# Layer 1 of a graph-network stack: the running-sum table built and read in two column ranges, both rows of a node in one gather

## The chip, the core and the metric

The kernel runs on one core of one Trainium2 chip. TensorE (PE) multiplies, VectorE (DVE), ScalarE (ACT) and GpSimd (POOL) do the element-wise work, SyncE (SP) and POOL issue transfers, and sixteen DMA engines move bytes between the chip's memory and on-chip memory. Each engine works through its own instructions in order and waits for the others by semaphores. The metric is the time on the device in microseconds, as the median of several runs.

## The reference, cut to what matters

Four graph layers run over 2708 nodes with 128 features each, all with the same adjacency matrix. Each begins with a layer norm and a relu, and adds to the residual `x`. The change is in layer 1 alone:

```python
XW = X @ W
s_col = XW @ a[0, :128];  s_row = XW @ a[0, 128:]
den = exp(leaky_relu(s_row[:, None] + s_col[None, :], 0.01))   # 2708 x 2708
num = A @ den
att = where(num != 0, den / num, 0)
H = A @ (att @ XW)
```

The product `A @ den` is the heavy part. Since `den[i, j]` is one exponential where `s_row[i] + s_col[j]` is positive and another where it isn't, column `j` of `num` is a sum over the nodes with a row term above a threshold, and another sum over those below. With the nodes sorted by `s_row` both come out of running sums over sorted rows of the adjacency matrix.

## The kernel before

The adjacency matrix comes in transposed (`adjT`), as rows of 2708 f32 values. Nodes go in 22 tiles of 128 (the last has 20), columns in six banks of 512 (the last has 148).

**Sorting.** The kernel counts for every node how many nodes lie ahead of it, writes pairs (node, row term) to their places in a list in memory (`order_d`), and reads the list back as `srtT`. The node numbers become the indices `src_u`.

**The table stage (L1492 to L1517).** Tile t of the running-sum table needs 126 rows of `adjT` in sorted order. `fetch` (L1399) gathers them with an indirect transfer that POOL issues, into one of four buffers `mov`, three tiles ahead. Rows 0 and 1 of a buffer carry the two running sums on from the tile before. For each bank TensorE multiplies the weights `wt` of the tile (128 x 128) with `mov` (L1498); VectorE copies the first two rows of the product from the accumulator into the next tile's buffer (L1502); and ScalarE, or VectorE for two of the six banks, copies the whole product to `knots` (L1503), which SP writes to the table in memory (L1515). One more column (2708) holds a running sum of weights. In the same loop ScalarE counts signs for the places of the nodes (`signs_of`, L1359), computes the weights of later tiles (L1458), and TensorE computes `xw` = XW (L362). The order of TensorE, VectorE and ScalarE here is partly pinned, partly chosen by a scheduler.

**The last pass (L1615 to L1627).** It starts when the whole table is written. For each node tile POOL gathers two table rows for each node, one below its threshold and one above (`lo` and `hi`, L1538), with one indirect transfer each. `interpolation` (L1546) computes a factor from the last column, `divided` (L1576) combines the rows on VectorE (L1584) and inverts the result on ScalarE by a logarithm and an exponential (L1588, L1589). One tile later `weighed` (L1591) multiplies by the numerator on VectorE (L1596), and TensorE accumulates the product with `xw` over all tiles in six banks (L1606).

**After it.** The accumulators are copied to `yT`, turned and scaled to `attended` (L1640), and `aggregate` (L370, products at L382) multiplies with `adjT` once more, whose rows SP loads in `chunk`s of one tile. The buffers of these chunks are those of `lo` and `mov`.

## Time and profile before

| What | Value |
|---|---|
| median of 3 runs | 1142.2 us (1142.18 to 1153.88) |
| the profiled execution's own time | 1143.4 us |
| its span, first to last instruction | 1141.7 us |
| mean granted TensorE clock | 0.947 |
| busy share of the span: PE, DVE, ACT, POOL | 88%, 53%, 36%, 21% |
| first product of the table stage (L1498) | 477.9 us |
| last table rows landed, first row gather issued | 640.3 us |
| first product of the last pass (L1606) | 661.7 us |
| last product of the last pass ends | 814.1 us |
| first product of the aggregation after it (L382) | 819.4 us |

The profile is one execution. Times of single instructions come from it, and the changed stretch is the 342 us between 477.9 and 819.4. In a table of groups each row is a line of the kernel, an engine and an operation, with count, busy time, mean duration in ns and the idle time before it with its cause. In a table of windows each row gives the busy time of the engines in one stretch, then the clock that TensorE was granted (1.00 is full speed), the mean share in which DMA engines had packets, and the bytes moved. Idle time of an engine that isn't the bound costs nothing.

### The profile page before, as it was taken

To read this page: it belongs to the slowest core of one execution; us is meant where nothing else is said; L and a number is where in the kernel's file an instruction comes from. 1 tells how busy PE (TensorE), PEld (TensorE's weight loads), DVE (VectorE), ACT (ScalarE), POOL (GpSimd) and SP (SyncE) were. 2 spreads that over 40 slices of the span, in tenths; PEclk is the share of its full clock that TensorE was granted. 3 is DMA by queue.
4 is the path that set the end of the run, shared out by engine and by line. 5 is a ranking of instruction groups with operands and counts; after the bars stand their busy time and mean duration, and the time that the engine had idled before them with its cause. 6 is when DMAs were issued, how large, how long until landed. Compare 5 with 4: busy or idle time off the path is not lost. (4 is left out here: it accounts for less than half of the span.)

```text
span 1141.7 us, 10167 instructions
## 1 busy us (share of the span) xinstructions
PE 1008.4 (88%) x3501; PEld 491.5 (43%) x3501; DVE 608.9 (53%) x1248; ACT 414.4 (36%) x660; POOL 237.5 (21%) x208
## 2 busy tenths in 40 slices
PE   7989999999989979777787177787999999999998
PEld 5444444443444455334343033333444455545444
DVE  4374369999823489366576389998500131122003
ACT  5010145555200267568574358877200130012000
POOL 2000000000477715411110447771000000000000
PEclk9989999999999979999899668888999999999999
DMA  9978120004598239799999799998599447725821
GB/s 288 348 269 265 38 80 1 1 29 166 217 388 355 53 112 408 232 367 409 367 375 374 261 424 424 422 413 342 227 383 321 177 148 254 280 98 180 307 98 49
DMA packets 52293, 284.00 MB, mean 249 GB/s; under 512 B 7535, under 2 KB 18918, under 8 KB 29794
## 3 DMA queue, kind: packets, MB, share of 16 engines
q1 hardware_dynamic: 37986, 188.96, 44.7%
q0 software_dynamic: 14016, 94.39, 21.6%
q8 instruction: 28, 0.46, 0.2%
q14 instruction: 23, 0.19, 0.0%
q10 hardware_dynamic: 240, 0.00, 0.0%
HBM read 250.98 MB, written 32.87 MB: 249 GB/s over the span
## 5 line engine op out<-in xcount | busy, mean ns | idle before, releaser
L1606 PE MATMUL acc<-hi,xw 128*128 128x512 f32 (+3 forms) x264 | 126.1, 641 | 55.2 <-DVE hi L1596 55.2
L382 PE MATMUL acc<-chunk,h 128*128 128x512 f32 (+1 forms) x384 | 148.0, 542 | 0.0
L1498 PE MATMUL acc<-mov,wt 128*128 128x512 f32 (+1 forms) x264 | 113.4, 582 | 32.9 <-DMA mov<-in_adj_dram,src_u 31.9
L900 POOL DMA_INDIRECT gath<-ydr,near_u x84 | 80.4, 957 | 191.5 <-issue 179.3
L779 PE MATMUL acc<-zT 128*128 128x512 f32 (+2 forms) x264 | 112.3, 559 | 0.0
L1606 PEld LDWEIGHTS acc<-hi,xw 128*128 128x128 f32 (+1 forms) x264 | 56.2, 222 | 125.1 <-issue 67.4
L1502 DVE COPY mov<-acc 2x512 f32<-2x512 f32 x126 | 74.2, 611 | 58.3 <-PE acc L1498 57.8
L382 PEld LDWEIGHTS acc<-chunk,h 128*128 128x128 f32 x384 | 68.8, 190 | 74.1 <-issue 74.1
L1498 PEld LDWEIGHTS acc<-mov,wt 128*128 128x128 f32 x264 | 51.1, 201 | 95.1 <-issue 71.6
L382 PE MATMUL acc<-chunk,y 128*128 128x512 f32 x204 | 79.9, 552 | 5.9 <-DMA chunk<-in_adj_dram 5.2
L794 ACT COPY strip<-acc 128x512 f32<-128x512 f32 (+1 forms) x132 | 60.4, 558 | 59.2 <-issue 35.8
L382 PE MATMUL acc<-chunk,attended 128*128 128x512 f32 x192 | 73.1, 542 | 2.8 <-DMA chunk<-in_adj_dram 2.8
L1503 ACT COPY knots<-acc 128x512 f32<-128x512 f32 x88 | 50.2, 588 | 56.3 <-DVE mov L1502 52.3
L1588 ACT ACTIVATE hi<-hi,lam 128x2708 f32<-128x2708 f32 (+3 forms) x24 | 56.5, 2363 | 35.0 <-issue 25.6
L796 DVE MAX8 top_v<-strip 128x8 f32<-128x2708 f32 (+1 forms) x22 | 64.6, 2963 | 7.3 <-ACT strip L794 7.3
L1538 POOL DMA_INDIRECT lo<-table,lo_u x22 | 55.2, 2511 | 61.8 <-issue 36.0
L1584 DVE SCALAR_TENSOR_TENSOR hi<-lo,lam,hi 128x2708 f32<-128x2708 f32 (+3 forms) x24 | 67.0, 2800 | 1.0
L779 PEld LDWEIGHTS acc<-zT 128*128 128x128 f32 (+1 forms) x264 | 45.1, 185 | 51.3 <-issue 43.8
L1596 DVE SCALAR_TENSOR_TENSOR hi<-row_all,inv_s,hi 128x2708 f32<-128x2708 f32 (+3 forms) x24 | 67.0, 2797 | 0.4 <-ACT hi L1589 0.4
L382 PEld LDWEIGHTS acc<-chunk,y 128*128 128x128 f32 x204 | 37.4, 193 | 48.4 <-issue 45.4
L1589 ACT ACTIVATE hi<-hi,hb 128x2708 f32<-128x2708 f32 (+3 forms) x24 | 56.5, 2362 | 0.7
L1362 ACT ACTIVATE sg<-row_all,c_nat 128x2708 bf16<-128x2708 f32 (+1 forms) x22 | 56.2, 2555 | 0.1
(323 smaller groups left out, 1280.6 us busy)
## 6 DMA issues: line engine op xcount, KB each, us to landing
chunk<-in_adj_dram SPq DMA_DIRECT2D x74, 1354.0 KB
table<-knots SPq DMA_DIRECT2D x20, 1354.5 KB
res<-in_adj_dram SPq DMA_DIRECT2D x9, 1354.0 KB
held<-in_adj_dram SPq DMA_DIRECT2D x11, 512.0 KB
held<-in_adj_dram SPq DMA_DIRECT2D x16, 256.0 KB
upper<-in_adj_dram SPq DMA_DIRECT2D x4, 842.0 KB
held<-in_adj_dram SPq DMA_DIRECT2D x3, 1024.0 KB
chunkY<-in_adj_dram SPq DMA_DIRECT2D x2, 1354.0 KB
```

What stands on the lines that cost most here:

```text
L382: nc.tensor.matmul(out[b][:, :n], y[r, i, :], chunk(i)[r, k0 : k0 + n], start=(i == 0), stop=(i == T - 2),)
L779: mm = nc.tensor.matmul(zz[b][:w, :n], zT[:, cols(t)], zT[:, k0 : k0 + n], start=True, stop=False)
L794: copied = nc.scalar.copy(s[:w, k0 : k0 + n], zz[b][:w, :n])
L796: nc.vector.max(top_v[:w, t, :], s[:w, :])
L900: nc.gpsimd.indirect_dma_start(out=g[: idx.shape[0], :], out_offset=None, in_=ydr[:, :], in_offset=bass.IndirectOffsetOnAxis(ap=idx, axis=0),)
L1498: nc.tensor.matmul(p[:, :n], wt[:, t, :], moving[t][:, k0 : k0 + n], start=True, stop=True)
L1502: nc.vector.tensor_copy(moving[t + 1][:2, k0 : k0 + n], p[:2, :n])
L1584: nc.vector.scalar_tensor_tensor(num, lo[:w, c], kap, num, op0=ALU.mult, op1=ALU.add)
L1588: nc.scalar.activation(num, num, AF.Ln, scale=sc)
L1589: nc.scalar.activation(num, num, AF.Exp, scale=-1.0, bias=hb40[:w, t : t + 1])
L1596: nc.vector.scalar_tensor_tensor(att[:w, c], row_all[:w, c], inv_s[:w, t : t + 1], att[:w, c], op0=ALU.max, op1=ALU.mult,)
L1606: nc.tensor.matmul(py[b][:, :n], xw[:w, t, :], att[:w, k0 : k0 + n], start=(t == T - 1), stop=(t == T - 2),)
```

## The change

The table is cut at column 1535 into two tables. The first covers columns 0 to 1534 and the column of weight sums (1536 wide), the second the other 1173 columns (1176 wide). Three stretches take the place of the table stage and the last pass.

1. The table stage runs over the first range alone: 22 tiles, three banks each. ScalarE copies bank 0 and VectorE banks 1 and 2. The two carried rows are copied from `knots`, no longer from the accumulator. Signs are counted here, five tiles ahead.
2. A loop over 22 tiles builds the second range's table (ScalarE copies two banks, VectorE the last of 152 columns). From its tile 3 on it issues gathers from the first table, and from its tile 6 on it does one item of the last pass: division ahead of the tile's knots, inversion and the weighing of the item before behind them. An item is a node tile in one range.
3. The other items, six of the first range and all 22 of the second, follow in a loop of their own, with gathers three items ahead.

A node's two table rows now always lie one after the other (each table tile has three carried or repeated rows, so a tile covers 125 nodes and no longer 126), and one indirect transfer brings both, as a row of twice the width. The index of a node's place is computed by rounding, no longer by comparison with all tile starts. All of these instructions are pinned in program order. The first range's half of `yT` and two groups of `attended` are computed inside the third stretch, and the first four chunks of the next aggregation go to new buffers that are free once the second table is made. The scaling and exponential of `row_all` stand between stretches 1 and 2. In front, a row of zeros is set after the indices are known, and the list is read back in two transfers.

```diff
-PER = P - 2
+PER = P - 3
...
-    big = ctx.enter_context(tc.tile_pool(name="big", bufs=4))
+    big_open = ExitStack()
+    big = big_open.enter_context(tc.tile_pool(name="big", bufs=4))
...
+    CUT = 3 * 512 - 1
+    PARTS = ((0, CUT, CUT + 1), (CUT, N, 4 * (-(-(N - CUT) // 4))))
+    WIDE = max(w for _, _, w in PARTS)
+    tables = [
+        dram.tile([P * (T - 1) + LAST, w], F32, name=f"table{h}") for h, (_, _, w) in enumerate(PARTS)
+    ]
...
-    first = row_place()
-    pin(nc.vector.memset(first[0:1, :N], 0.0))
-    nc.vector.memset(first[:, N : N + 1], 0.0)
-    nc.vector.memset(first[0:1, N : N + 1], 1.0)
...
-    for t in range(4):
+    for t in range(5):
...
-    nc.gpsimd.dma_start(srtT[:, 2:, :], order_d[: T * PER, :].rearrange("(t f) c -> t f c", f=PER))
+    for a_, e_, c in ((1, 1 + T * PER, slice(3, P)), (0, T * PER, slice(2, 3))):
+        nc.gpsimd.dma_start(
+            srtT[:, c, :],
+            order_d[a_:e_, :].rearrange("(t f) c -> t f c", f=PER)[:, : c.stop - c.start, :],
+        )
...
+    l1.close()
+    rows_open.close()
+    big_open.close()
+    made = ExitStack()
+    moved = made.enter_context(tc.tile_pool(name="moved", bufs=4))
+    knots = made.enter_context(tc.tile_pool(name="knots", bufs=3))
+    moving = {}
+    tots = keep.tile([P, QUARTER], F32, name="tots", tag="own")
...
+    def fetch(h, t):
+        c0, c1, w = PARTS[h]
+        n = c1 - c0
+        m = moving[h, t] = moved.tile([P, WIDE], F32, name="mov", tag="mov")
+        if t == 0:
+            dve.memset(m[0:1, :n], 0.0)
+        dve.memset(m[:, n:w], 0.0)
+        if t == 0 and h == 0:
+            dve.memset(m[0:1, n:w], 1.0)
+        pin(
...
+    def total_row(h):
+        c0, c1, _ = PARTS[h]
+        for g in range(4):
+            a_, e_ = max(c0, QUARTER * g), min(c1, QUARTER * (g + 1))
...
+    def make_knots(h, t, bank, on_act):
+        m = moving.pop((h, t))
+        o = knots.tile([P, WIDE], F32, name="knots", tag="knots")
+        p = [acc(bank + x_) for x_, _, _ in pieces(h)]
+        for x_, a_, e_ in pieces(h):
+            pe.matmul(p[x_][:, : e_ - a_], wt[:, t, :], m[:, a_:e_], start=True, stop=True)
+        for x_, a_, e_ in pieces(h):
+            if x_ in on_act:
+                act.copy(o[:, a_:e_], p[x_][:, : e_ - a_])
+        for x_, a_, e_ in pieces(h):
+            if x_ not in on_act:
+                dve.tensor_copy(o[:, a_:e_], p[x_][:, : e_ - a_])
+            if t < T - 1:
+                dve.tensor_copy(moving[h, t + 1][:2, a_:e_], o[:2, a_:e_])
+        n = P if t < T - 1 else LAST
+        w = PARTS[h][2]
+        pin(nc.sync.dma_start(tables[h][t * P : t * P + n, :], o[:n, :w]))
+
+    def ahead_fetch(h, t):
+        if t < T:
+            fetch(h, t)
+        elif h == 0:
+            fetch(1, t - T)
+            if t == T:
+                total_row(1)
+
     for t in range(T):
-        if t + 3 < T:
-            fetch(t + 3)
-        o = rowtile("knots")
-        for b, (k0, n) in enumerate(EKBS):
-            p = acc(b)
-            nc.tensor.matmul(
-                p[:, :n], wt[:, t, :], moving[t][:, k0 : k0 + n], start=True, stop=True
-            )
-            if t < T - 1:
-                nc.vector.tensor_copy(moving[t + 1][:2, k0 : k0 + n], p[:2, :n])
-            (nc.vector.tensor_copy if b in (2, 5) else nc.scalar.copy)(o[:, k0 : k0 + n], p[:, :n])
-        if t + 4 < T:
-            signs_of(t + 4)
-        if t == T - 4:
+        ahead_fetch(0, t + 3)
+        make_knots(0, t, 3 * (t % 2), (0,))
+        if t + 5 < T:
+            signs_of(t + 5)
+        if t == T - 5:
             row_places()
         if t % 4 == 0 and t // 4 + 1 < NG:
             weights(t // 4 + 1)
         if t % 3 == 2 and t // 3 < NG:
-            node_product(hT, wg, t // 3, keep_xw, behind=True)
-        s0 = 0 if t else 2
-        if t < T - 1:
-            for c in (slice(0, HALF), slice(HALF, N + 1)) if t == 0 else (slice(0, N + 1),):
-                nc.sync.dma_start(table[t * P + s0 : (t + 1) * P, c], o[s0:, c])
-    for c in (slice(0, HALF), slice(HALF, N + 1)):
-        nc.sync.dma_start(table[(T - 1) * P : (T - 1) * P + LAST, c], o[:LAST, c])
-
-
-    pin(nc.vector.tensor_scalar(row_all, row_all, rmax, 0.99, op0=ALU.subtract, op1=ALU.mult))
-    pin(nc.scalar.activation(row_all, row_all, AF.Exp, bias=forty))
+            weighted(t // 3)
...
+    dve.tensor_scalar(row_all, row_all, rmax, 0.99, op0=ALU.subtract, op1=ALU.mult)
+    act.activation(row_all, row_all, AF.Exp, bias=forty)
...
+    pairs = between.enter_context(tc.tile_pool(name="pairs", bufs=4, side="right"))
+    atts = between.enter_context(tc.tile_pool(name="atts", bufs=4, side="right"))
...
+    def gather(h, t):
+        w, n = width(t), PARTS[h][2]
+        r = pairs.tile([P, 2 * WIDE], F32, name="pair", tag="pair")
+        rows[h, t] = r[:, :n], r[:, n : 2 * n]
+        pin(
+            nc.gpsimd.indirect_dma_start(
+                out=r[:w, : 2 * n],
+                out_offset=None,
+                in_=tables[h][:, :],
+                in_offset=bass.IndirectOffsetOnAxis(ap=pair_u[:w, t : t + 1], axis=0),
+            )
...
+    ORDER = [0, T - 1, *range(1, T - 1)]
+    SETS = {0: (0,), T - 1: (T - 1,), **{t: (t, t + 1) for t in range(1, T - 1, 2)}}
+    WORK = [(h, t) for h in range(2) for t in ORDER]
+    gathers, work = list(WORK), list(WORK)
...
+    def divided(h, t):
+        w = width(t)
+        if h == 0 and t in SETS:
+            interpolation(SETS[t])
+        lo, hi = rows.pop((h, t))
+        at = attention[h, t] = atts.tile([P, WIDE], F32, name="att", tag="att")
+        for c in cuts(h, t):
+            dve.scalar_tensor_tensor(
+                at[:w, c], lo[:w, c], kap[:w, t : t + 1], hi[:w, c], op0=ALU.mult, op1=ALU.add
+            )
...
+    def weighed(h, t):
+        w = width(t)
+        at = attention.pop((h, t))
+        c0, c1, _ = PARTS[h]
+        for c in cuts(h, t):
+            dve.scalar_tensor_tensor(
+                at[:w, c],
+                row_all[:w, c0 + c.start : c0 + c.stop],
+                inv_s[:w, t : t + 1],
+                at[:w, c],
+                op0=ALU.max,
+                op1=ALU.mult,
+            )
+        if h not in py:
+            py[h] = [acc(3 * h + x_) for x_ in range(3)]
...
+    waiting = []
+    for t in range(T):
+        if t + 3 < T:
+            fetch(1, t + 3)
+        if t >= 3:
+            gather(*gathers.pop(0))
+        now = work.pop(0) if t >= 6 else None
+        if now:
+            divided(*now)
+        make_knots(1, t, 3, (0, 1))
+        if now:
+            inverted(*now)
+        if waiting:
+            weighed(*waiting.pop())
+        if now:
+            waiting.append(now)
+    made.close()
...
-    sets = [(T - 1,)] + [(t,) for t in range(3)] + [(t, t + 1) for t in range(3, T - 1, 2)]
-    assert sets[-1][-1] == T - 2
-    before = []
-    for ts in sets:
-        for t in ts:
-            fetch_rows(t)
-        interpolation(ts)
-        for t in ts:
-            divided(t)
-            if before:
-                weighed(before.pop())
-            before.append(t)
-    weighed(before.pop())
...
+    LEAD = 3
+    while work:
+        while gathers and len(gathers) > len(work) - 1 - LEAD:
+            gather(*gathers.pop(0))
+        now = work.pop(0)
+        divided(*now)
+        inverted(*now)
+        before = waiting.pop()
+        weighed(*before)
+        if before == (0, ORDER[-1]):
+            y_turned(0)
+        if before[0] == 1 and before[1] in (ORDER[1], ORDER[4]):
+            attend_early(0 if before[1] == ORDER[1] else 1)
+        if len(work) == 2:
+            for i in range(2):
+                resident[i] = chunk(i)
+        waiting.append(now)
+    weighed(*waiting.pop())
+    between.close()
...
-            if i == 0:
-                for g in range(min(lead + 1, NG)):
-                    step(g)
-            elif i % 4 == 0 and i // 4 + lead < NG:
+            if i and i % 4 == 0 and i // 4 + lead < NG:
...
```

## The prediction

> **What bounds the kernel now.** The chain of waits comes first: it leads back from the end through layer 2's adjacency products at 819.4 us, the last pass of layer 1 and its row gathers. The change touches only 472 to 819 us, so I cut that stretch into windows (columns: window, length, then busy time and instructions of PE, PEld, DVE, ACT, POOL; granted clock, DMA share, GB/s).

> ```profile
> 500.00:540.00 40.00, 32.12 (x105) 16.82 (x104) 27.46 (x63) 30.64 (x42) 6.83 (x7) 1.00 1.01 411
> 632.00:641.00 9.00, 0.99 (x4) 0.38 (x2) 1.85 (x2) 3.64 (x3) 0.74 (x1) 0.71 0.71 250
> 641.00:650.00 9.00, 0.00 (x0) 0.00 (x0) 2.91 (x8) 0.29 (x1) 6.87 (x8) 0.50 0.77 241
> 700.00:750.00 50.00, 40.34 (x91) 18.35 (x91) 48.90 (x52) 40.59 (x24) 37.34 (x16) 0.90 1.00 418
> ```

> The table stage (first row) is held by DMA: 22 tiles from 477.9 to 633 us, 7.0 us each, 2.75 MB each (fetch and table write). Rows two and three are the seam: for 29 us, until 661.7, no TensorE product starts. The last pass (fourth row) has VectorE full, and DMA too. The timeline of VectorE gives its pace:

> ```profile
> 721.91 3.04 DVE L1584 SCALAR_TENSOR_TENSOR hi<-lo,lam,hi 128x2708 f32<-128x2708 f32 x1
> 724.87 3.03 DVE L1596 SCALAR_TENSOR_TENSOR hi<-row_all,inv_s,hi 128x2708 f32<-128x2708 f32 x1
> 727.82 3.03 DVE L1584 SCALAR_TENSOR_TENSOR hi<-lo,lam,hi 128x2708 f32<-128x2708 f32 x1
> 730.76 3.03 DVE L1596 SCALAR_TENSOR_TENSOR hi<-row_all,inv_s,hi 128x2708 f32<-128x2708 f32 x1
> 735.30 3.04 DVE L1584 SCALAR_TENSOR_TENSOR hi<-lo,lam,hi 128x2708 f32<-128x2708 f32 x1
> ```

> Starts lie 2.95 us apart, and four of them plus 1.58 us of interpolation make 13.39 us for two tiles: 6.69 us a tile. A seam can be filled only if the engines in the filled stretch don't wait for each other; the durations for that come from the groups by form and from TensorE's timeline.

> ```profile
> L1498 PE MATMUL acc<-mov,wt 128*128 128x512 f32 x219 | 107.8, 641 | 32.9 <-DMA mov<-in_adj_dram,src_u 31.9 <-ACT knots L1503 1.0
> L1502 DVE COPY mov<-acc 2x512 f32<-2x512 f32 x105 | 69.5, 675 | 58.3 <-PE acc L1498 57.8
> L1503 ACT COPY knots<-acc 128x512 f32<-128x512 f32 x87 | 49.7, 588 | 56.0 <-DVE mov L1502 52.3 <-PE acc L1498 3.4
> L1503 DVE COPY knots<-acc 128x149 f32<-128x149 f32 x21 | 6.1, 292 | 0.0
> L1596 DVE SCALAR_TENSOR_TENSOR hi<-row_all,inv_s,hi 128x1536 f32<-128x1536 f32 x2 | 3.6, 1817 | 0.4 <-ACT hi L1589 0.4
> ```

> ```profile
> 541.72 4.78 PE L1498 MATMUL acc<-mov,wt 128*128 128x512 f32 x12 [1.49 <-DMA mov<-in_adj_dram,src_u]
> 549.73 6.48 PE L1498 MATMUL acc<-mov,wt 128*128 128x512 f32 x12 [3.23 <-DMA mov<-in_adj_dram,src_u]
> 557.67 4.79 PE L1498 MATMUL acc<-mov,wt 128*128 128x512 f32 x12 [1.47 <-DMA mov<-in_adj_dram,src_u]
> 566.53 6.48 PE L1498 MATMUL acc<-mov,wt 128*128 128x512 f32 x12 [3.18 <-DMA mov<-in_adj_dram,src_u]
> ```

> The same twelve matmuls take 4.79 us after a pause of 1.5 us and 6.48 after one of 3.2: a pause costs 1.69 us of slow clock. In the last pass pauses of 2.3 us already cost it.

> **The change, part by part.** *Start.* A second read of the order (POOL, 0.9 us) and the memset of one row, now behind the index cast on VectorE (2.31 us for 2708 columns at L1347, so 1.3), stand ahead of the first fetch, less what they overlap: it goes from 472.1 to 473.7, the first product from 477.9 to 479.5.

> *First range* (1535 columns). Per tile 0.77 MB fetched and 0.79 written. The table stage moved 376 GB/s on the mean from 480 to 620: 4.15 us. ScalarE needs a sign pass (2.68 start to start), a copy (0.65) and, every fourth tile, four weight passes (1.50): 3.7 us. VectorE needs two copies of 0.67 and three 2-row copies, which now read SBUF: no row shows that copy. Its bounds are 0.68 (the PSUM row above) and 0.3 (L1520 passes 2708 SBUF columns in 1.62 us, 0.6 ns each); I take 0.45, nearer the lower, since that row's source is the same: 2.8 us. DMA leads; with some jitter 4.25 us x 22 = 93.5, end at 573.

> *Second range beside the first of the last pass.* DMA: fetch 13.0, write 13.2, nineteen gathers (one of 20 rows) 28.6 MB; at 395 GB/s (between 376 and the last pass's 420) 139 us, 6.9 us a tile in full swing. The orders on the engines ask for more. TensorE does tile t's knots, then weighs item k-1; VectorE does item k's division, the 2-row copies of tile t, then the weighing of k-1. So weighing k-1 on VectorE precedes its products, these precede the knots of t+1, those precede ScalarE's copies, those the 2-row copies, and behind them stands weighing k. This is a ring: weighing 1.82; three products 2.58 (ten matmuls in 4.29 us on the chain, two to a product); two knots products 1.72; from a product's end to its reader 0.27 (first matmul 477.94, first copy 479.07); ScalarE's copy 0.59; 2-row copy 0.45, the 152-column piece 0.29 and its 2-row copy 0.27; six handovers 0.2. Sum 8.2 us. Division, interpolation and logarithms fit beside it.

> Within it TensorE works 4.56 us and pauses 3.6. [...] By the rows 3.2 us is enough each time: 8.2 + 1.69 = 9.9 us. I take the rows, since the pause lies above theirs.

> The ring turns 15 times: 148 us. Ahead of it come tile 0 with row_all's scale and exponential (1.62 + 2.55 us, once in the seam), 5 us; five tiles without a gather in their way (1.19 MB, 3.1 us), 15.5; one without weighing, 4.5. In all 173 us, to 746.

> *Rest of the last pass.* VectorE: 13 operations of 1535 columns at 1.74 (1.82 less the overlap of 0.08 seen above) 22.6; 44 of 1173 at 1.35 (the 1172-column form takes 1.43) 59.4; three interpolations 4.7; eight early attend scalings at 0.34 and a copy 3.4; small waits for ScalarE (2.51 of each 2.70 us) 4: 94 us. DMA has 30.2 MB of gathers and 5.5 of early chunk loads, 85 us at 420: beneath it. POOL issues one gather per item; it takes 2.65 us under an operation of VectorE and 0.94 free, and gets in at the boundary between two, of which each item has two. End at 840, the first product of layer 2 at 841.3 with no evacuation between (before: 814.1 to 819.4). That is 21.9 later; layer 2's wait for chunks (2.8 us at L382) goes, since four are loaded.

> *At nothing:* node places without the comparison table (1.1 + 1.1 us of VectorE inside the DMA-held stage; uncovered they would save 2), PER 125 instead of 126 (still 22 tiles), signs five ahead, pool moves.

> Sum: 21.9 - 2.8 = +19.1. The profiled execution took 1143.4 us (span 1141.7), 1.2 above the median 1142.2, so 1161 against the median.

> **The rivals.**
> *The clock holds* in the ring: 15 x 8.2, 25 us less: 1136. [...]
> *DMA is the bound* and the ring slack: were the second range to run at its 139 us, 34 less: 1127, faster. This is the other side: one mechanism, queues kept full by three fetches and three gathers ahead; it decides where the ring falls below 6.9 us, 1.3 under its warm sum. For it, DMA share 1.00 in both stages; against, both in-order engines.
> *The first range stretches:* from 478 to 490 us, with fetches alone on the queue, the trace shows 219 to 283 GB/s. If writes of smaller pieces leave the fetches alone for half the time, 34.3 MB go at 300: 114 instead of 93.5 us, 1181. For it the low start; against it 411 from 500 to 540.

> **How the numbers follow.** Forecast 0.50 (1150 to 1172: the 2-row copies at 0.3 to 0.68 are -4 to +7 us, the first range's jitter and the rest of the pass 4 each); clock holds 0.17 (1131 to 1150); DMA bound 0.13 (below 1131); stretched first range 0.20 (1172 to 1195). The range 1133 to 1180 leaves out about 0.13 below and 0.07 above. Under 1% of change this kernel's measurements can't be told from none. Faster 0.13, same 0.20 (the clock case and the forecast's lowest end), slower 0.67.

> **What would show it.** Right: in the second range TensorE's bursts every 9.9 us with a pause near 3.6 before each, released by the weighing; granted clock near 0.7 to 0.8; DMA share clearly below 1; VectorE waiting for ScalarE's knots copies; before it a tile every 4.25 us, after it VectorE full for 94 us. Wrong: pauses of TensorE that end with a fetch or a gather (then DMA bounds), or a clock of 1.0 there. What would break the number most is a 2-row copy far from 0.45, or a gather that comes late for its division.

## The result, and the profile after

The changed kernel takes **1185.95 us** (median of 4 runs, 1185.75 to 1187.65) where the kernel before took 1146.81 us beside it (4 runs, 1142.18 to 1153.88): 1.034 times as long, with a 95% interval of 1.027 to 1.041. The prediction said 1161 us, with a range of 1133 to 1180. The sign was right, the size was not: the loss is more than twice the one forecast.

Both profiled executions can be cut at the same points: the last product of the first aggregation, in which the code did not change; the first knots product; the last weighing product; and the last product of layer 2's first aggregation. In the changed kernel the second range starts where VectorE begins to scale `row_all`, and the rest of the pass starts where the last knots product ends.

| Stretch, us | before | after | difference | forecast |
|---|---|---|---|---|
| up to the end of the first aggregation | 377.1 | 380.6 | +3.4 | 0 |
| from there to the first knots product | 100.8 | 105.2 | +4.4 | +1.6 |
| knots to the last weighing product | 336.4 | 372.9 | +36.5 | +24.1 |
| of this: first range | | 86.2 | | 93.5 |
| second range | | 171.1 | | 173 |
| rest of the last pass | | **115.6** | | **94** |
| from there to layer 2's last product | 107.6 | 106.0 | -1.7 | -6.6 |
| profiled span | 1141.7 | 1184.2 | +42.5 | +19.1 |

The first row is no effect of the change. In the eleven kernels with the new tables, the same up to that point, it lies between 375.5 and 382.7 us from one profiled execution to the next. The lengths of the later stretches agree much better where the code is the same (in the three kernels below that share both stretches, 147.6 to 148.0 us for the second range and 96.0 to 96.3 for the rest of the pass), so the experiments are read by stretches. An exception is the first range of the first experiment, 3 us longer without an edit there.

The windows of the changed kernel, with the columns as in the prediction (window, length, busy time and instructions of PE, PEld, DVE, ACT, POOL, then granted clock, DMA share, GB/s). They show the first range, the second, and three pieces of the rest of the pass:

```profile
486.00:572.00 86.00, 76.93 (x214) 30.55 (x213) 59.35 (x145) 61.59 (x74) 22.82 (x22) 1.00 1.01 370
600.00:743.00 143.00, 92.17 (x174) 39.63 (x174) 81.03 (x180) 62.92 (x60) 46.17 (x27) 0.81 0.87 313
743.00:770.00 27.00, 15.70 (x31) 5.94 (x30) 18.85 (x33) 16.07 (x11) 9.03 (x4) 0.89 0.91 365
770.00:800.00 30.00, 22.10 (x44) 9.57 (x45) 23.58 (x27) 18.52 (x15) 13.59 (x7) 0.76 0.77 275
830.00:858.00 28.00, 22.35 (x62) 10.71 (x61) 25.50 (x21) 23.73 (x21) 9.45 (x5) 1.00 0.69 284
```

The first range is DMA's, as forecast. In the second no engine is full, and DMA isn't either (0.87): something goes round in a circle there. This mean hides two parts:

```profile
600.00:637.90 37.90, 20.95 (x31) 8.52 (x31) 19.34 (x46) 15.43 (x14) 8.50 (x7) 0.64 1.01 355
637.90:743.00 105.10, 71.22 (x144) 31.11 (x144) 61.70 (x135) 47.50 (x47) 37.67 (x21) 0.87 0.82 298
```

Up to 637.9 us DMA is full (1.01); only behind that is it not (0.82), and there the circle turns. In the rest of the pass VectorE should be full; it is only in the last piece. From 743 to 770 us it is busy for 18.85 of 27 us.

TensorE's timeline shows the circle (start, duration, what it computes, how many, and in brackets the pause ahead of it and who ended it):

```profile
657.01 4.27 PE L85 MATMUL acc<-att,xw 128*128 128x512 f32 x6 [3.08 <-DVE att L85]
661.07 2.45 PE L85 MATMUL acc<-mov,wt 128*128 128x512 f32 x6
666.60 2.84 PE L85 MATMUL acc<-att,xw 128*128 128x512 f32 x6 [3.08 <-DVE att L85]
669.28 2.14 PE L85 MATMUL acc<-mov,wt 128*128 128x512 f32 x6
674.50 4.54 PE L85 MATMUL acc<-att,xw 128*128 128x512 f32 x6 [3.08 <-DVE att L85]
```

Each weighing (`att,xw`) comes after a pause of 3.08 us that VectorE's weighing ends, and the knots (`mov,wt`) follow without one. A turn takes 9.5 to 9.6 us where the six matmuls take 4.2 us or more, and 7.9 us where they take 2.84. The ring is there. The 2-row copy, whose cost no row of before showed, is among the groups by form:

```profile
L85 DVE COPY mov<-knots 2x512 f32<-2x512 f32 x105 | 44.6, 426 | 91.9 <-ACT knots L85 90.4
```

426 ns each, where the forecast took 0.45 us; and VectorE waits for ScalarE's copies in front of them.

For the rest of the pass the waits tell most. VectorE's own, from 743.0 to 858.5 us (who waited, for whom; us in total, times, longest):

```profile
DVE attended L85 <- PE ps L85: 8.6, 2, 4.6
DVE lam L85 <- DMA pair<-table,pair_u: 7.7, 2, 6.7
DVE yT L85 <- PE acc L85: 3.9, 2, 2.1
DVE knots L85 <- PE acc L85: 3.2, 1, 3.2
DVE att L85 <- ACT att L85: 0.9, 2, 0.7
```

The wait ahead of `knots` ended at 743.1 us and so lies before the stretch. The others add up to 21 us, where the forecast had 4. The two largest are things that the change put into the pass: the scalings of layer 2 (`attended`), which wait for TensorE's transposes, and gathers (`pair`) that are late. The timeline places them, with what was issued at the same time:

```profile
749.18 2.16 SPq L99 DMA_DIRECT2D chunk<-in_adj_dram  x4
...
769.93 0.21 DVE L85 TENSOR_SCALAR lam<-pair 128x1 f32<-128x1 f32 x1 [6.67 <-DMA pair<-table,pair_u]
...
793.77 1.12 DVE L85 TENSOR_SCALAR attended<-ps,wk 128x128 f32<-128x128 f32 x4 [4.00 <-PE ps L85]
794.17 6.26 PE L392 MATMUL acc<-chunk,attended 128*128 128x512 f32 x10 [0.44 <-DVE attended L85]
...
807.67 1.13 DVE L85 TENSOR_SCALAR attended<-ps,wk 128x128 f32<-128x128 f32 x4 [4.58 <-PE ps L85]
```

The chunks are issued at 749 us, over 90 us before the code that asks for the first two of them: SP had nothing ahead of them, and their buffers were free. Also to be seen: ten matmuls of layer 2's own products at 794 us, inside the pass, since their operands were ready.

### The profile page after: what moved, and what is told of

It is laid out like the page before. It is cut to its first block, busy times and chain, and to the rows that moved or that the text cites. A ratio compares the mean times of both kernels' runs of the same rounds, so it can differ in the third digit from the quotient of the medians.

```text
span 1184.2 us, 10366 instructions
## 1 busy us (share of the span) xinstructions
PE 1030.9 (87%) x3501; PEld 490.7 (41%) x3501; DVE 602.0 (51%) x1328; ACT 410.2 (35%) x659; POOL 254.0 (21%) x229
## 2 busy tenths in 40 slices
DMA packets 58635, 284.53 MB, mean 240 GB/s; under 512 B 8655, under 2 KB 20039, under 8 KB 41278
## 3 DMA queue, kind: packets, MB, share of 16 engines
q0 software_dynamic: 17408, 94.69, 22.6%
## 4 chain that ended last, share of the span: by engine, by line
PE 59%; DMA 16%; issue 11%; DVE 7%; POOL 5%; ACT 1%; POOLq 0%; SPq 0%; DVEq 0%; ACTq 0%
PE acc L392 27%; PE acc L85 14%; PE acc L789 9%; DMA chunk<-in_adj_dram 5%; DMA pair<-table,pair_u 5%; DVE att L85 4%; DMA mov<-in_adj_dram,src_u 3%; POOL pair L1563 2%; PE ps L85 2%; POOL mov L1408 2%; PE ps L1310 1%; PE ps L372 1%; DMA held<-in_adj_dram 1%; PE acc L797 1%; PE acc L303 1%
## 5 line engine op out<-in xcount | busy, mean ns | idle before, releaser
L85 PE MATMUL acc<-att,xw 128*128 128x512 f32 (+4 forms) x264 | 134.2, 657 | 79.5 <-DVE att L85 79.5
L392 PE MATMUL acc<-chunk,h 128*128 128x512 f32 (+1 forms) x384 | 148.0, 542 | 0.0
L85 PEld LDWEIGHTS acc<-att,xw 128*128 128x128 f32 (+1 forms) x264 | 54.2, 219 | 147.1 <-DVE att L85 91.6
L1563 POOL DMA_INDIRECT pair<-table,pair_u x44 | 86.9, 1976 | 93.0 <-DVE att L85 87.6
L85 DVE COPY mov<-knots 2x512 f32<-2x512 f32 (+1 forms) x126 | 50.3, 400 | 92.7 <-ACT knots L85 90.4
L392 PE MATMUL acc<-chunk,attended 128*128 128x512 f32 (+1 forms) x192 | 78.2, 564 | 7.0 <-DMA chunk<-in_adj_dram 6.6
L1408 POOL DMA_INDIRECT mov<-in_adj_dram,src_u x44 | 47.9, 1089 | 141.7 <-PE acc L85 127.1
L85 ACT ACTIVATE att<-att,sca 128x1535 f32<-128x1535 f32 (+5 forms) x45 | 63.0, 1399 | 37.8 <-DVE att L85 37.5
L85 DVE SCALAR_TENSOR_TENSOR att<-pair,kap 128x1535 f32<-128x1535 f32 (+5 forms) x45 | 71.6, 1592 | 1.1 <-DMA pair<-table,pair_u 0.4
L85 DVE SCALAR_TENSOR_TENSOR att<-row_all,inv_s,att 128x1535 f32<-128x1535 f32 (+5 forms) x45 | 70.6, 1571 | 0.9 <-ACT att L85 0.9
L85 ACT ACTIVATE att<-att,hb 128x1535 f32<-128x1535 f32 (+5 forms) x45 | 63.0, 1399 | 1.5
```

What stands on the lines that cost most here:

```text
L85: return lambda *a, **k: pin(getattr(self.engine, name)(*a, **k))
L392: nc.tensor.matmul(out[b][:, :n], y[r, i, :], chunk(i)[r, k0 : k0 + n], start=(i == 0), stop=(i == T - 2),)
L1408: nc.gpsimd.indirect_dma_start(out=m[2:, :n], out_offset=None, in_=adjT[:, :], in_offset=bass.IndirectOffsetOnAxis(ap=src_u[:FROM, t : t + ...
L1563: nc.gpsimd.indirect_dma_start(out=r[:w, : 2 * n], out_offset=None, in_=tables[h][:, :], in_offset=bass.IndirectOffsetOnAxis(ap=pair_u[:w, ...
```

## The experiments

The theory from the traces has four separate causes: (1) the ring holds the second range, and a slow clock lengthens it; (2) early chunk loads delay gathers in the rest of the pass; (3) the early scalings make VectorE wait there; (4) the overlap itself earns little. Each was changed alone, then together. All lengths are from the profiled executions, in us.

| Kernel | to first knots | first range | second range | rest of pass | layer 2 | median | ratio to before (95%) |
|---|---|---|---|---|---|---|---|
| changed | 105.2 | 86.2 | 171.1 | 115.6 | 106.0 | 1186.0 | 1.034 (1.027 to 1.041) |
| weighing first | 104.8 | 89.3 | **150.7** | 108.9 | 106.0 | 1157.6 | 1.011 (1.005 to 1.018) |
| late chunks | 104.8 | 86.8 | 170.3 | **107.0** | 108.4 | 1177.4 | 1.029 (1.024 to 1.034) |
| scalings after | 105.4 | 85.6 | 168.7 | **107.1** | 107.9 | 1175.5 | 1.026 (1.021 to 1.031) |
| no overlap | 105.2 | 86.2 | **88.2** | **182.1** | 102.8 | 1163.6 | 1.018 (1.012 to 1.024) |
| three edits | 105.2 | 86.7 | 147.6 | 96.3 | 111.2 | 1148.0 | 1.002 (1.000 to 1.004) |
| no overlap, two edits | 104.8 | 86.2 | 88.3 | 165.9 | 108.5 | 1152.2 | 1.006 (1.003 to 1.008) |
| warm ring | 105.3 | 85.5 | **158.3** | 116.0 | 106.6 | 1171.5 | 1.015 (1.007 to 1.022) |
| start reordered | 104.9 | 91.4 | 148.0 | 96.0 | 110.3 | 1149.4 | 1.004 (1.002 to 1.006) |
| totals first | 103.9 | 88.3 | 147.6 | 96.3 | 103.3 | 1144.1 | 1.001 (0.997 to 1.005) |

"Layer 2" runs from the last weighing product to the last product of its first aggregation.

### The weighing taken out of the ring

```diff
+        if waiting:
+            factored(*waiting[-1])      # VectorE's half of weighed(k-1)
         make_knots(1, t, 3, (0, 1))
         if now:
             inverted(*now)
         if waiting:
-            weighed(*waiting.pop())
+            summed(*waiting.pop())      # TensorE's half
```

> In the second range the weighing of item k-1 goes ahead of tile t's copies on VectorE; its products stay where they are on TensorE. Nothing is left out. Theory (the ring through weighing, products, knots and copies sets 171 us of the second range): the weighing leaves the ring, the turn falls from 9.6 or 7.9 us towards DMA's 6.9, TensorE's pauses of 3.1 us before the weighing products go or end with a DMA or a knots copy, the second range falls to 140 to 150 us, and the kernel to 1156 to 1168 us. Rival (the second range is held by late gathers and fetches, and the ring only fills what they leave): the range stays within 5 us of 171, the kernel at 1180 to 1190.

The second range fell from 171.1 to 150.7 us, just above the 140 to 150 expected, and the kernel to 1157.58 us. The windows of this kernel show what took the ring's place:

```profile
600.00:640.00 40.00, 26.47 (x48) 11.36 (x47) 23.65 (x55) 17.89 (x17) 12.13 (x8) 0.69 1.02 350
640.00:720.00 80.00, 57.50 (x125) 25.90 (x125) 55.57 (x118) 43.23 (x41) 32.75 (x19) 0.83 1.00 357
```

DMA is full now to the end, at 350 to 357 GB/s (before the edit: 0.87 and 313 on the mean, 0.82 and 298 from 637.9 us on). VectorE's waits from 600 to 720 us are for it: 24.1 us for gathers. The rival, that late transfers were the cause and the ring only filled what they left, is out: a new order on VectorE alone took 20 us away. DMA is the next bound, 22 tiles in 150.7 us = 6.85 us a tile. The rest of the pass fell too, by 6.7 us to 108.9, though no line of it was edited: VectorE's waits in it shrank together, from 21.5 to 14.8 us.

### The chunks behind the last gather

```diff
         while gathers and len(gathers) > len(work) - 1 - LEAD:
             gather(*gathers.pop(0))
+            if not gathers:
+                for i in range(4):
+                    resident[i] = chunk(i, nc.gpsimd)   # issued by GpSimd
...
-        if len(work) == 2:
-            for i in range(2):
-                resident[i] = chunk(i)
```

> The four chunks of layer 2 are loaded from GpSimd's queue behind the last gather instead of from SP's queue at 749 us. Nothing is left out. Theory A (the chunks' 5.5 MB stood in front of gathers, 7.7 us of VectorE's wait at 762 to 770 us): that wait goes, the rest of the last pass falls from 115 to about 107 us. Theory B (layer 2's first products ran inside the last pass and held TensorE): they can't run before their chunks land, so another 4 to 5 us go, to about 103 us. Both together: the kernel at 1172 to 1178 us, with no more than 3 us given back in layer 2. Rival (the gathers are late because VectorE frees their buffers late, whatever else is on the queues): the rest of the pass stays above 112 us, the kernel above 1182.

The rest of the pass fell by 8.6 us to 107.0, and 2.4 came back in layer 2. VectorE's waits in it (737.6 to 844.5 us):

```profile
DVE attended L85 <- PE ps L85: 8.3, 2, 5.5
DVE yT L85 <- PE acc L85: 3.9, 2, 2.1
```

The 7.7 us for gathers are gone, which rules out the rival that VectorE frees the buffers late. The wait for the transposes is as long as it was (8.3 against 8.6), although layer 2's products have moved behind the pass: so theory A holds, and the part of theory B that blamed these products falls. The transfers explain it. In the changed kernel, from 743 to 770 us (issues: bytes, median us to landing):

```profile
chunk<-in_adj_dram SPq DMA_DIRECT2D x4, 1354.0 KB
...
pair<-table,pair_u POOLq DMA_INDIRECT x4, 18.1
```

and from 770 to 858 us, with no chunk on the way:

```profile
pair<-table,pair_u POOLq DMA_INDIRECT x20, 9.2
```

A gather landed after 9.2 us when no chunk was on the way and after 18.1 beside 5.4 MB of chunks, though those were issued from another queue. The trace has the landing of four of the twenty gathers and of two of the four; in the kernel with the late chunks the median is 8.6 us from 738 to 845 us. A queue of their own was no protection for the gathers here.

### The early scalings behind the pass

```diff
-        if before[0] == 1 and before[1] in (ORDER[1], ORDER[4]):
-            attend_early(0 if before[1] == ORDER[1] else 1)
...
     weighed(*waiting.pop())
+    for g in range(2):
+        attend_early(g)
```

> The two early groups of layer 2's scalings (8 transposes, 8 scalings of 0.28 us) come after the last weighing instead of inside the pass; with them layer 2's first products move behind the pass. The chunks stay early. Nothing is left out. Theory B (VectorE waits 4.0 and 4.6 us in the pass for these transposes, because TensorE must first finish the weighing products, and layer 2's products hold it longer): the rest of the last pass falls from 115 to about 104 us, 2.5 of it being the scalings themselves; the seam to layer 2 grows by 4 to 5 us; the kernel at 1178 to 1182 us. Theory A (chunks alone): the pass stays at 112 us or more, and the kernel grows to 1187 or more.

The rest of the pass fell by 8.5 us to 107.1 (104 was expected) and layer 2 grew by 1.9; the kernel came to 1175.45 us, somewhat better than expected, since the seam costs 2 us and not 4 to 5. VectorE's waits from 738.4 to 845.5 us:

```profile
DVE lam L85 <- DMA pair<-table,pair_u: 7.4, 2, 7.2
DVE yT L85 <- PE acc L85: 3.5, 1, 3.5
```

The mirror image: the wait for transposes is gone and the one for gathers stays. On VectorE, `attended` stood right behind the weighing; its transposes stand behind that weighing's products on TensorE. VectorE thus waits for TensorE to finish all products of the item that it has only just handed over: in the changed kernel twelve matmuls of two weighings fill TensorE from 787.10 to 793.15 us, and the scalings start at 793.77. The eight scalings themselves take 2.3 us; the waiting took 8.6.

### No overlap

```diff
-        if t >= 3:
+        if 3 <= t < 7:
             gather(*gathers.pop(0))
-        now = work.pop(0) if t >= 6 else None
+        now = None
```

> The two ranges, the pair gathers and the early chunks stay, but no item of the last pass runs beside the second range: the range makes its 22 tiles alone, then 44 items follow (the first four gathers go out in the second range). Nothing is left out. Theory (the shared ring costs more than it hides): alone a tile is product 1.7, copy 0.6 and 0.3, 2-row copy 0.4 and 0.3, handovers, 3.5 us, so the range takes 75 to 82 us in place of 171; the 15 items that it had beside it cost 15 x 4.3 us on VectorE behind it, so the pass takes 115 + 65 = 180 us; in sum 20 to 35 us faster, 1151 to 1166 us. Rival (the overlap pays as it was meant to): the range still takes over 110 us alone, or the pass grows by more than 90 us; the kernel at 1190 us or more.

The two ranges alone, with all 44 items behind them, are faster than the changed kernel: 1163.56 us against 1186. The second range takes 88.2 us, more than the 75 to 82 expected (from 572 us on the DMA share is 0.96, with four gathers in it), the pass 182.1. Together 270.3, against 286.7 with the overlap. The overlap as it was built, with the ring in it, costs 16 us.

### The three edits together, with and without overlap

> The three edits of the first experiments together: the weighing first on VectorE, the chunks of layer 2 behind the last gather, the early scalings behind the pass. Nothing is left out. Theory (ring, late gathers and the waits for the transposes are separate causes, and the second range is then held by DMA at some 355 GB/s): second range 150 us, rest of the last pass 94 to 100 us instead of 115, layer 2 to its last product 107 to 110; the kernel at 1143 to 1150 us, level with the kernel before. Rival (the causes overlap: with the ring gone, gathers are late again in the pass because DMA is behind): the rest of the pass stays above 105 us, the kernel at 1155 or more.

1147.97 us, against 1145.99 of the kernel before: level. The rest of the pass is 96.3 us, and VectorE's waits in it (722.2 to 818.5 us) are:

```profile
DVE yT L85 <- PE acc L85: 2.1, 1, 2.1
DVE knots L85 <- PE acc L85: 1.9, 1, 1.9
DVE att L85 <- DMA pair<-table,pair_u: 1.2, 2, 1.0
DVE att L85 <- ACT att L85: 0.8, 2, 0.6
```

The one ahead of `knots` lies before the stretch; the others come to 4 us, as much as the forecast for this stretch had supposed. The causes nearly add up. Late chunks and late scalings took 8.6 and 8.5 us when each was alone, which leaves 98.5 of 115.6; the weighing first had taken 6.7 alone, which would leave 91.8; 96.3 was measured. The shares of the three overlap, then, by some 4.5 us.

The same two edits on the pass, without any overlap:

> No item of the last pass beside the second range, with the late chunks and the late scalings as well. Nothing is left out. Theory (an item costs DMA in the second range what it costs VectorE in the pass, 1.57 MB at 355 GB/s = 4.4 us against 4.3 us, so with the waits cleared it makes little difference where it runs): second range 88 us, the pass 165 to 170 us in place of 182; the kernel at 1145 to 1154 us, within 8 us of the one with the three edits. Rival (the overlap, once its ring is open, earns its 58 us of VectorE work): this kernel is over 20 us behind the one with the three edits.

1152.22 us. The pass is 16.2 us shorter than without the two edits (182.1), near the sum of the two, 17.1, with no ring at all. First knots to last weighing takes 340.4 us here and 330.6 with overlap, so the overlap earns 10 us once its ring is open (the medians differ by 4; layer 2 takes 2.7 us less here): it shortens the pass by 69.6 us (165.9 to 96.3) and lengthens the range by 59.3 (88.3 to 147.6). The reason is in the windows of the two (the second range without overlap; then the second range with it):

```profile
572.00:659.80 87.80, 57.97 (x130) 26.17 (x128) 29.52 (x106) 26.89 (x46) 24.84 (x23) 0.83 0.95 344
```

```profile
600.00:722.00 122.00, 85.66 (x178) 38.16 (x177) 83.45 (x189) 64.45 (x62) 46.84 (x28) 0.79 1.02 366
```

DMA is nearly full in the range without the items (0.95) and full with them (1.02). An item brings a gather of 1.57 MB, 4.3 us at 366 GB/s, and spares VectorE two operations of 1.8 us and 0.8 of interpolation, 4.4 us. What is taken from the pass is paid for in the range.

### The clock in the ring

The order of the changed kernel, with eight spare products in TensorE's pause:

```diff
         make_knots(1, t, 3, (0, 1))
+        if waiting:
+            warm(acc(5), 8)
```

> Eight spare 128x512 bf16 products, whose result nothing reads, stand in TensorE's pause ahead of each weighing in the second range; the order is that of the changed kernel. Nothing is left out. Theory (the pause of 3.1 us halves the clock in two turns of three, 1.7 us each): all turns take 7.9 us, TensorE's weighing products 2.8 us instead of 4.5, the second range falls from 171 to 155 to 160 us and the kernel to 1168 to 1175 us. Rival (the slow clock is hidden, another engine or DMA ends the turns): the second range stays at 168 us or more.

```profile
675.34 2.84 PE L85 MATMUL acc<-att,xw 128*128 128x512 f32 x6
678.02 2.14 PE L85 MATMUL acc<-mov,wt 128*128 128x512 f32 x6
681.24 1.89 PE L303 MATMUL acc<-ident_b 128*128 128x512 bf16 x8 [1.09 <-DVE knots L85]
683.23 2.84 PE L85 MATMUL acc<-att,xw 128*128 128x512 f32 x6
```

From 635.9 us on every turn takes 7.89 us and every weighing's matmuls 2.84 us; the second range fell by 12.8 us to 158.3, the kernel to 1171.49. Work that computes nothing made the kernel 14 us faster. In the changed kernel eight of the twelve weighings from 637.9 us on had come at the slow clock; eight times 1.69 us is 13.5.

```profile
634.39:637.80 3.41, 0.42 (x3) 0.19 (x1) 2.55 (x6) 3.17 (x3) 2.39 (x2) 1.00 0.90 332
637.80:641.21 3.41, 3.32 (x4) 1.51 (x5) 3.08 (x13) 0.46 (x1) 0.88 (x1) 0.50 1.04 385
661.69:665.10 3.41, 1.83 (x6) 0.76 (x4) 1.56 (x5) 2.38 (x3) 1.05 (x1) 1.00 0.54 227
665.10:668.52 3.42, 1.92 (x5) 0.96 (x6) 3.18 (x3) 1.83 (x2) 3.35 (x1) 1.00 0.82 258
668.52:671.93 3.41, 2.90 (x9) 1.23 (x7) 0.53 (x2) 1.32 (x3) 0.83 (x2) 1.00 0.80 264
```

The first pause lies almost whole in one step, in which TensorE is busy for 0.42 us, and the next step has half the clock (0.50). The second is divided between two steps, and the clock stays (1.00). Of the 31 steps from 634.4 to 740.2 us, 23 have the full clock. Eight of them have TensorE idle for 62% or more, and each is followed by a step at half clock; the other 15 are idle for 56% or less, and none is. In the trace of the kernel before, from 500 to 815 us, the two groups lie at 63% and more and at 54% and less. The division is not complete: in the changed kernel the step from 791.40 to 794.81 us, filled mostly with the products of the item of 20 rows, is idle for 13% and was followed by half clock too.

### One range, one gather

The single gather alone: `PARTS = ((0, N, N + 1),)`, no second range, all items behind the table.

> One part of the change alone: a single range of 2708 columns, no overlap, but both rows of a node in one gather of 21.7 KB, its own tile for the division and four gathers in flight; layer 2's chunks can't be loaded before the pass ends here, for want of room, so the time from there on isn't comparable. Nothing is left out. Theory (the harm lies in the two ranges and in what was put into the pass, not in the single gather): table stage 155 us as before, then 29 us of seam, then the pass; from the first knots product to the last weighing product 330 to 340 us, where the kernel before takes 336 and the changed one 373. Rival (the single gather itself is slow, its rows land late or hold VectorE up): over 345 us.

From the first knots product to the last weighing product it takes 333.8 us, 2.5 less than before. So the single gather is neither the harm nor a gain to speak of. (The kernel takes 1157.62 us; its chunks come after the pass.)

### The start of the table stage

The copy of the sorted values and the weights' steps ahead of the memsets (on top of the three edits):

> The three edits together, and the start of the table stage as well: the copy of the sorted values and the three steps of the weights go ahead of the memsets of the first fetch on VectorE and ahead of the copies of the totals on ScalarE. Nothing is left out. Theory (the first product waits for the weights, which stand behind 1.5 us of memsets and 0.9 us of the totals, and not for the fetch): from the end of the first aggregation to the first knots product 102 to 103.5 us instead of 105.2 (the kernel before 100.8); the kernel 2 to 3 us below the one with the three edits, 1143 to 1147 us, level with the kernel before. Rival (the product waits for the fetch, which starts as late as ever): still 105 us, 1147 to 1150.

Neither came: 1149.39 us, first knots after 104.9 us, and the first range 91.4 instead of 86.7. TensorE's timeline of this kernel:

```profile
485.87 1.10 PE L85 MATMUL acc<-mov,wt 128*128 128x512 f32 x2 [2.10 <-DMA mov<-tots]
...
491.36 3.69 PE L85 MATMUL acc<-mov,wt 128*128 128x512 f32 x4 [4.39 <-DMA mov<-tots]
```

The weights were in time, but now the total row was late. Its small loads (three, up to 2.6 KB each) went out at 480.75 us, behind two fetches; the last product that needs them ran at 491.36. So the totals went first in the next kernel, and with that the residents of layer 2 (six chunks kept for later layers) were loaded one at a time instead of three at once, ahead of chunk 4:

```diff
     dve.tensor_copy(rs, p[:, T : 2 * T])
+    # totals (two copies, two steps), then pw, nw, kn
     for t in range(3):
         fetch(0, t)
...
-    ... back=3, first=3
+    ... back=3, first=1
```

> The three edits, with the start ordered so that the totals and then the weights go ahead of the first memsets on VectorE, and layer 2's six resident chunks loaded one at a time instead of three at its start. Nothing is left out. Theory (the first product of the table stage waits for the last of weights and totals; layer 2 waits 5 us for chunk loads because 4 MB of residents stand ahead of them): from the end of the first aggregation to the first knots product 102 to 104 us instead of 105.2, first range 86 to 88 us, layer 2's waits for chunks under 2 us instead of 5.1; the kernel at 1139 to 1145 us, up to 0.5% below the kernel before. Rival (the start is set by the readback of the order and by the first fetch, and the residents' loads only move): no change from the kernel with the three edits, 1146 to 1150 us.

1144.09 us, against 1143.59 of the kernel before: no difference. The start gained 1.3 us (103.9). Layer 2 gained 7.9 (103.3). TensorE's timeline of the kernel with the three edits shows what was lost there:

```profile
877.55 25.59 PE L392 MATMUL acc<-chunk,attended 128*128 128x512 f32 x60 [4.93 <-DMA chunk<-in_adj_dram]
```

and of this one:

```profile
861.55 22.88 PE L392 MATMUL acc<-chunk,attended 128*128 128x512 f32 x60
```

The waits for chunks fell from 5.1 to 1.0 us in all, and the sixty matmuls behind the longest of them take 2.7 us less, at a granted clock of 1.00 where it was 0.90 behind the long wait. The two parts of this edit can't be told apart by the median; by stretches they can. No version was found that beats the kernel before by more than its runs differ (1143.6 to 1146.8 us are its medians beside the single kernels).

## Why the prediction was right on the sign and wrong on the size

**The step that failed** is "Rest of the last pass", 94 us: it took 115.6. VectorE's work in it was sized well (93.0 us busy against 90 without the waits). What failed was the term "small waits for ScalarE (2.51 of each 2.70 us) 4". ScalarE did cost only 0.9 us; the other 20 us of waits were for others. "DMA has 30.2 MB of gathers and 5.5 of early chunk loads, 85 us at 420: beneath it" set a sum over the whole stretch against its length, and did not ask when the chunks go out. All four went out at 749 us, beside gathers issued at 748.6 and 752.0 that VectorE was ready to use at 762 and 763 us: it waited 7.7 us. "Eight early attend scalings at 0.34" counted their execution and not the wait that they bring, with VectorE standing still until TensorE had done what was queued there: 8.6 us. The copies of the first range to `yT` waited 3.9 us more. The chunks and the scalings were moved one at a time, and with both moved and the ring gone 96.3 us remained.

**"Layer 2's wait for chunks (2.8 us at L382) goes, since four are loaded"** was wrong too: it grew to 6.6 us. Three residents of 1.35 MB each are issued ahead of chunk 4. The stretch came out 4.9 us above its forecast.

**The ring** was right in its order, its pauses (3.08 us against 3.6) and the 2-row copy. That 171.1 us stand against 173 is in part luck, since two errors cancel. Up to the knots of tile 7 the range took 30 us instead of 25, and the first two turns took 12.2 and 16.7 us; in the second VectorE waited 8.8 us for a gather that took 25 us to land (594.3 to 619.3) while DMA was full. In exchange the regular turns, all forecast at 9.9 us with the slow clock, took 9.12 on the mean over eleven (637.89 to 738.25): two in three had the slow clock (9.59), the others took 7.90.

The rival "clock holds" fell for this kernel, and the warm ring shows what it would have been worth: 12.8 us of the second range. Its chance was the author's estimate. That the length of a pause decides ("3.2 us is enough each time", and 2.3 us in the last pass) was read from too few rows: two pauses in the table stage of before, of 2.56 and 2.91 us, did not cost the clock, and the twelve matmuls behind each took 4.78 us:

```profile
507.81 4.78 PE L1498 MATMUL acc<-mov,wt 128*128 128x512 f32 x12 [2.56 <-DMA mov<-in_adj_dram,src_u]
616.37 4.78 PE L1498 MATMUL acc<-mov,wt 128*128 128x512 f32 x12 [2.91 <-DMA mov<-in_adj_dram,src_u]
```

So neither "each time" nor "the clock holds" was right for the ring. Pauses of 3.08 us gave the slow clock in eight of twelve cases, pauses of 1.09 us in none.

**"DMA is the bound"** gave the second range 139 us were the ring open; with the ring open it took 147.6 to 150.7, at 350 to 369 GB/s instead of 395.

**First range**: 86.2 us instead of 93.5. The rate was not better than supposed: 370 GB/s, where 376 was taken. But only 31.9 MB moved in the stretch (370 GB/s in 86.2 us) and not 34.3 (22 tiles of 0.77 and 0.79 MB), since the first fetch goes out at 477.1 us, ahead of the first product at 485.8; and the 2.2 us put down for jitter were not needed. The rival "stretches" fell.

**Start**: the first fetch came 1.5 us later (measured from the end of the first aggregation), as forecast. The first product came 4.4 us later. The memset was put ahead of the fetch in the sum, where it hides; on VectorE it also stands ahead of the copy from which the weights are made. The products for the weights start 3.5 us behind the index cast (475.97 to 479.48), where it was 1.3 before (470.98 to 472.28), and the fourteen spare products that TensorE runs next took 4.59 us instead of 3.79. The experiment that moved the weights shows that the total row is next in line.

Against the forecast these come to: start +2.8, first range -7.3, second range -1.9, rest of the pass +21.6, layer 2 +4.9, and +3.4 of the stretch that didn't change: +23.5, where the spans give 42.5 - 19.1 = 23.4.

## What to carry to other kernels

Before work is moved beside other work, ask which resource the place is already full of: here the stage that was to be filled was DMA's (a share of 0.95 without the items), and the items brought their own transfers along. When an instruction is put early into an in-order engine, count what it waits for and not only how long it runs; the scalings, placed directly behind their own producer's handover, waited for the whole of that producer's queue (4.0 and 4.6 us, to run for 2.3). A load with a free buffer and a free queue may go out long before its place in the program text (here over 90 us); if it must not collide, put it behind the transfers that it must not pass.

## What the runs showed of the hardware that was not expected

- Gathers took 18.1 us to land instead of 9.2 while 5.4 MB from another queue were on the way (medians of two and four gathers; 8.6 us from 738 to 845 us in the kernel with the late chunks).
- Three loads of a few KB, issued behind two gathers of 0.77 MB each, held the first tile up until 10.6 us after their issue (480.75 to 491.36).
- Equal pauses of 3.08 us were followed by the slow clock in eight turns and by the fast one in four. In the ring it went by where a pause lay on the steps of 3.41 us at which the clock of this trace changed: 62% or more of one step idle, and the next had half the clock (0.50); 56% or less, and it kept it (1.00).
- The two ranges move the same bytes as one (284.5 MB in the whole kernel, before 284.0) in more packets: 58,635 against 52,293, and 41,278 under 8 KB against 29,794. In the second range, with the ring open, full DMA moved 350 to 369 GB/s, where the old table stage moved 389 from 500 to 620 us. That the smaller rows are the reason was not tried.
